# VectorE's read of one kept number takes a second operand from PSUM, at every step of left too, and not in the first 64 steps

## The chip, the cores and the metric

The kernel runs on one core of one Trainium2 chip. The metric is the time of one execution on the device, in microseconds. Besides plain runs, one execution was taken by the hardware profiler; its records are the trace, and a page summed up from them is the profile. Engines are named as in the profile: PE is TensorE's matmuls, PEld its weight loads, DVE is VectorE, ACT is ScalarE, POOL is GpSimd, SP is SyncE, which here only starts DMA transfers.

## The reference

The input `x` has the shape (4, 48, 256, 256) in float32: four images of 48 channels. Four layers are applied, each ahead of a normalization over all of an image and with the layer's input added to its output:

- Layer 0: attention between the channels, after a 3x3 depthwise convolution of queries, keys and values.
- Layer 1: a small gated unit with a depthwise convolution.
- Layers 2 and 3: "spatial message passing". The image is gone through row by row from the top (down), then from the bottom (up), then column by column from the left (right) and from the right (left). Each row or column is replaced by itself plus a convolution along it (5 taps, 48 channels to 48, and a bias) of the row or column before it, whose new value it uses: `nxt = inp + conv1d(carry)`.

The scans of layers 2 and 3 take most of the time, and what is changed lies in them. Within one direction a row can't begin before the row ahead of it is done. So a scan is a chain of some 255 small steps, four scans make a layer, and two layers follow each other.

## The kernel before, in words

**How a step is laid out.** The function `scans` (L965) works through layers 2 and 3, which it calls layer 0 and layer 1. The four images form two pairs, and each pair has its own chain, a Python generator (`chain`, L1019) that emits one step of its pair at each `yield`. Even and odd positions of a row are folded onto the partitions, so that the 48 channels become 96 partitions and the 256 positions 128, and the five taps become three matrices of 96x96. A step (`step`, L1056) treats the two images of its pair as two halves, i = 0 and i = 1. For each half, three matmuls accumulate in a PSUM tile (L1064, float32, each of two records in the trace), and VectorE adds the row of the input and writes the result to one of four `carry` tiles (L1068 in down and up, L1072 in right and left). The first half of a pair uses one PSUM bank, the second half another; each is used again at the next step. So the next step's matmuls of a half wait for the add of the same half.

**What follows a step.** The function `after` of each scan stores what the step made:

- down (L1134 to L1157): ScalarE adds the bias and writes the row in place (`keep`, L1150).
- up (L1167 to L1201): the same, at L1194.
- right (L1252 to L1298): GpSimd fetches a column out of the block ahead of time (`fetch`, L1256, the copy at L1259; two steps ahead for pair 0, three for pair 1 with its additional tile), and ScalarE writes the new column to `lines` (L1286).
- left (L1315 to L1405): GpSimd adds the new column to the image that the layer started from. In pair 1 of the last layer (`direct`) it adds half by half into tiles `done` (L1338); otherwise once per step in place into `stage` (L1334). In layer 0, VectorE takes the statistics for the next normalization from a finished block (bn_stats, L1376), one piece per step of the next block, eight pieces a block. `CB` is 16 columns, `NK` is 16 blocks.

**The read of one kept number.** After each step of down, up and right the function `look` (L1030) is called with a place of one number per partition in the tile that ScalarE (or GpSimd) has just written. It appends the place to the list `kept`. When the list is longer than three it takes the oldest, three steps old, and lets VectorE copy that number to a tile `seen` that nobody uses (L1039). In right the number is added to one of the column fetched for the next step, so that the instruction reads both (L1041). In left, at odd columns outside `direct`, VectorE copies a number of the odd column before, which GpSimd has written (L1344 to L1348). What `seen` holds plays no part in the result. The read makes VectorE wait at that place for the other engine, so that a later instruction on VectorE needs no wait of its own for it. `kept` is emptied at each block of 32 rows in down and up, and once ahead of right and of left.

**What sets the order.** The engines' instruction orders are decided by a scheduler of the framework when the program is built: instructions carry a priority by their place in the Python program, and an instruction may be moved ahead of others if its inputs come earlier in the plan. A tile that is reused makes the next writer wait for its last reader. The chains are run at L1453 to L1473: first pair 0 alone for 992 steps, with pair 1 beginning 64 steps ahead of the end of these; then both in turns; and at the end pair 1 alone, while GpSimd rearranges pair 0's result (`to_rows`, L1421, its copies at L1448). So pair 0 is alone in its first layer, both pairs are interleaved in the middle, and pair 1 is alone in most of its second layer.

Of the kernel before, what the change touches and what calls it, by code (L numbers as in the profile page):

```python
# [9 lines left out]
F32 = mybir.dt.float32  # L10
AF = mybir.ActivationFunctionType
ALU = mybir.AluOpType
# [4 lines left out]
B, C, H, W = 4, 48, 256, 256  # L17
G = 16
NP = 2
P = 96  # L20
# [944 lines left out]
def scans(ctx, tc, xs, out, wts, biases, dram, k, coefs, lead, spare):  # L965
# [13 lines left out]
    nc = tc.nc  # L979
# [8 lines left out]
    wp = pool("c_w", 1)  # L988
# [10 lines left out]
    CB = 2 * KC  # L999
# [19 lines left out]
    def chain(pair):  # L1019
# [4 lines left out]
            nc.gpsimd.memset(c, 0.0)  # L1024
        last = wp.tile([P, 2, W // 2], F32, tag=f"last{pair}", name=f"last{pair}")
        at = [0]
        seen = wp.tile([P, 1], F32, tag=f"seen{pair}", name="seen")
        kept = []

        def look(place, fetched=None):  # L1030

            kept.append(place)
            if len(kept) > 3:
                if fetched is None:
                    nc.vector.tensor_copy(seen, kept.pop(0))  # L1039
                else:  # L1040
                    nc.vector.tensor_add(seen, kept.pop(0), fetched)  # L1041

        def slot(name):
            return take(pair, f"{name}{pair}")

        def inner():
            return carry[at[0]][:, :, 1 : HP - 1]

        def advance():
            at[0] = (at[0] + 1) % NC  # L1050
            return inner()
# [4 lines left out]
        def step(layer, way, inp, after):  # L1056

            old = carry[at[0]]
            new = advance()
            for i in range(2):  # L1060
                b = slice(i, i + 1)
                ps = sums[pair].tile([P, 512], F32, tag="bank", name=f"ps{pair}{i}")[:, : W // 2]
                for j in range(3):
                    nc.tensor.matmul(  # L1064
                        ps, lhsT=w_sb[layer][:, way, j, :], rhs=old[:, i, j : j + W // 2], start=j == 0, stop=j == 2
                    )
                if len(inp.shape) == 4:
                    nc.vector.tensor_add(  # L1068
                        new[:, i].rearrange("p (k w) -> p k w", w=KC), ps.rearrange("p (k w) -> p k w", w=KC), inp[:, i]
                    )  # L1070
                else:
                    nc.vector.tensor_add(new[:, i], ps, inp[:, i])  # L1072
                after(new, b)

        def rows_view(t):
            return t.rearrange("p (b k h w) -> p b k h w", b=2, k=NK, w=KC)
# [8 lines left out]
        def row(ts, r):  # L1085
            return rows_view(ts[r % 2])[:, :, :, r // 2, :]
# [13 lines left out]
        def layer_of(layer, first):  # L1100
# [18 lines left out]
            def norm(t, b):  # L1119
                v = by_batch(t)[:, b]  # L1120
                g = biased[b]
                nc.scalar.activation(v, v, AF.Identity, bias=g[:, 1:2], scale=g[:, 0:1])
# [11 lines left out]
            for n in range(NT):  # L1134
                ahead_ = None
                for r in range(RT):
                    if r == 0:
                        kept.clear()
                        while len(halves) < min(2 * n + 5, 2 * NT):
                            t = slot("dn")  # L1140
                            load_rows(layer, len(halves) // 2, len(halves) % 2, t, 0, NK)
                            halves.append(t)
                        if n + 1 < NT:
                            ahead_ = halves[2 * n + 2 : 2 * n + 4]
                    if ahead_ and r in (11, 14, 22, 25):
                        norm(ahead_[r // 22], r % 11 // 3)
                    inp = row(now, r)

                    def keep(new, b):
                        nc.scalar.activation(inp[:, b], blocks(new[:, b]), AF.Identity, bias=bias[:, 0:1])  # L1150

                    if n == 0 and r == 0:
                        keep(inner(), slice(0, 2))
                    else:
                        step(layer, 0, inp, keep)
                    look(inp[:, 1, 0, 0:1])
                    yield  # L1157
                if ahead_:
                    for r in range(2):
                        nc.sync.dma_start(D[n][r], now[r])  # L1160
                    now = ahead_
# [5 lines left out]
            for n in reversed(range(NT)):  # L1167
                ahead_ = None
                kept.clear()
                for r in reversed(range(RT)):  # L1170
# [17 lines left out]
                    i = n * RT + r + 1  # L1188
# [63 lines left out]
            fetched = {}  # L1252
# [59 lines left out]
            direct = layer == 1 and pair == NP - 1  # L1312
            done = None
            writes = []
            for n in reversed(range(NK)):  # L1315
                ahead_ = None
                if direct and n % 2 == 1:
                    done = [take(0, "done") for _ in range(2)]
                for w in reversed(range(CB)):
                    if w == CB - 1 and n > 0:  # L1320
                        ahead_ = slot("lines"), slot("stage")
                        nc.sync.dma_start(ahead_[0], Rt[n - 1])
                        nc.sync.dma_start(by_batch(ahead_[1]), block_of(x, n - 1))
                    if layer == 0 and n == 0 and w == CB // 2:
                        following = [slot("dn"), slot("dn")]
                        for r in range(2):
                            load_rows(1, 0, r, following[r], 1, NK)
                    line = lines_view(lines)[:, w]
                    to = cols_view(stage)[:, :, w % 2, :, w // 2]

                    def keep(new, b):
                        if not direct:
                            if b.stop == 2:
                                nc.gpsimd.tensor_add(to, to, new)  # L1334
                            return
                        for i in range(b.start, b.stop):
                            place = done[i].rearrange("p (h w) -> p h w", w=2 * CB)[:, :, n % 2 * CB + w]
                            nc.gpsimd.tensor_add(place, to[:, i], new[:, i])  # L1338

                    if n == NK - 1 and w == CB - 1:  # L1340
                        keep(inner(), slice(0, 2))
                    else:
                        step(layer, 2, line, keep)
                    if not direct and w % 2:  # L1344

                        kept.append(to[:, 1, H // 2 - 1 :])
                        if len(kept) > 1:
                            nc.vector.tensor_copy(seen, kept.pop(0))  # L1348
                    if late:
                        late.pop(0)()  # L1350
                    if writes and w % 8 == 4:
                        writes.pop(0)()
                    yield
                if layer == 0:
                    nc.sync.dma_start(block_of(y, n), by_batch(stage))
                elif not direct:
                    v = stage.rearrange("p (b q t n) -> p b q t n", b=2, q=2, t=NY)
                    for b in range(2):
                        for q in range(2):
                            nc.sync.dma_start(result[:, b, :, 2 * n + q], v[:, b, q])  # L1360
                elif n % 2 == 0:

                    def write(b, r, done=done, w0=n * CB):
                        at_rows = out[(2 * pair + b) * C : (2 * pair + b + 1) * C].rearrange(
                            "c (h r w) -> c h r w", r=2, w=W
                        )
                        nc.sync.dma_start(
                            at_rows[:, :, r, w0 : w0 + 2 * CB],
                            done[b][r * C : (r + 1) * C].rearrange("c (h w) -> c h w", w=2 * CB),
                        )  # L1370

                    writes += [lambda b=b, r=r, f=write: f(b, r) for b in range(2) for r in range(2)]
                if layer == 0:

                    def stat(b, c, n=n, v=by_batch(stage)):
                        nc.vector.bn_stats(stats[b][:, n * 4 + c, :], v[:, b, c * 512 : (c + 1) * 512])  # L1376

                    late += [lambda b=b, c=c, f=stat: f(b, c) for b in range(2) for c in range(4)]
                    if n == 0:
                        for r in range(2):  # L1380
                            for q in range(2):
                                nc.sync.dma_start(
                                    rows_view(following[r])[q * C : (q + 1) * C, :, 0].rearrange("c b h w -> c b (h w)"),
                                    cols_view(stage)[r * C : (r + 1) * C, :, q, :NH, :].rearrange("c b h w -> c b (h w)"),
                                )
                if ahead_:
                    lines, stage = ahead_
# [211 lines left out]
```

## Time and profile before

| what | value |
|---|---|
| median of three runs | 9098.82 us (9097.15 to 9113.03) |
| the profiled execution itself | 9105.24 us |
| its span, first to last instruction | 9103.5 us |
| mean granted TensorE clock | 0.984 |
| busy PE / DVE / ACT / POOL | 96% / 44% / 38% / 21% |
| matmul records at L1064 | 48,960 |
| looks at L1039 / L1041 / L1348 | 1,852 / 1,008 / 381 |

The layers 0 and 1 end near 3,500 us. Then come pair 0 alone (down, up, right, left of its first layer) until about 5,000 us, both pairs until about 7,640 us, and pair 1 alone until the end, with its last right from about 8,366 us and its last left from about 8,740 us.

A line of the groups in the profile reads: line of the kernel, engine, operation, output and inputs by their names in the program, the shapes, the count, then the busy time of all in us and the mean duration in ns of one, then the idle time ahead of them on their engine and what ended most of it. Four of them that concern the change, two from the page and two from the list of groups by form:

```profile
L1041 DVE TENSOR_TENSOR seen<-lines,pre 96x1 f32<-96x1 f32 x1008 | 166.8, 165 | 479.6 <-POOL pre L1259 437.2 <-ACT lines L1286 2.3 <-DVE seen L1041 0.2
L1348 DVE COPY seen<-stage 96x1 f32<-96x1 f32 x381 | 57.0, 150 | 306.3 <-POOL stage L1334 306.3
L1039 DVE COPY seen<-dn 96x1 f32<-96x1 f32 x1040 | 148.1, 142 | 33.6 <-ACT dn L1150 19.8 <-ACT dn L1194 2.1
L1376 DVE BATCH_NORM_STATS2 st<-stage 96x6 f32<-96x512 f32 x256 | 174.3, 681 | 7.4 <-POOL stage L1334 7.3
```

The idle time ahead of the looks is spread over all stages. Where TensorE is full it costs nothing.

### The profile page before, as it was taken

Reading aid. Unit: us, or ns where it says so; the run is one execution under the profiler, and the core shown is the slowest. Engines: PE = TensorE matmul, PEld = TensorE weight load, DVE = VectorE, ACT = ScalarE, POOL = GpSimd, SP = SyncE. Lnnn points to the kernel's source line nnn. Section 1 sums busy time; section 2 is a strip of 40 time slices with the busy share of each in tenths; the row PEclk is TensorE's granted clock in tenths of the full one; section 3 lists DMA queues with packets and bytes.
Section 4 is the critical chain, followed back from the end, with each engine's and each line's share of the span. In section 5 each row is a group of like instructions: output and inputs, shape, how many; then the busy total and the mean of one; then the engine's idle time right before and its main releaser. Section 6 shows DMA issues by size and latency. Waiting matters only on the chain. (4 is left out here: it accounts for less than half of the span.)

```text
span 9103.5 us, 158554 instructions
## 1 busy us (share of the span) xinstructions
PE 8713.5 (96%) x62920; PEld 7234.4 (79%) x62920; DVE 3971.3 (44%) x14031; ACT 3440.2 (38%) x7023; POOL 1948.2 (21%) x3100
## 2 busy tenths in 40 slices
PE   6999999999999978999999999999999999999998
PEld 4777777433333336999888999999999999999998
DVE  3232010234555555444345544444444555444543
ACT  0011000123343455765400776666554002765610
POOL 0000000001111120002444000001445664001566
PEclk9999999999999988999999999999999999999999
DMA  7664323467878877765466755465556787867789
GB/s 150 132 133 89 71 62 73 94 137 168 180 171 179 180 159 163 161 143 143 119 168 165 168 140 135 116 152 134 161 158 163 215 224 175 204 168 191 210 171 184
DMA packets 1180201, 1390.37 MB, mean 153 GB/s; under 512 B 263184, under 2 KB 1107216, under 8 KB 1118784
## 3 DMA queue, kind: packets, MB, share of 16 engines
q1 hardware_dynamic: 1179360, 1379.90, 64.9%
q8 instruction: 493, 8.08, 0.4%
q14 instruction: 252, 2.06, 0.1%
q0 software_dynamic: 96, 0.33, 0.0%
HBM read 811.21 MB, written 509.61 MB: 145 GB/s over the span
## 5 line engine op out<-in xcount | busy, mean ns | idle before, releaser
L1064 PE MATMUL ps<-carry,w 96*96 96x128 f32 x48960 | 5490.2, 274 | 115.0 <-DVE carry L1072 71.7
L1064 PEld LDWEIGHTS ps<-carry,w 96*96 96x96 f32 x48960 | 5407.4, 163 | 207.4 <-DVE carry L1072 134.7
L1259 POOL COPY pre<-col 96x256 f32<-96x256 f32 x1020 | 656.7, 644 | 2755.5 <-DMA col<-last 1971.7
L1150 ACT ACTIVATE dn<-carry,b 96x128 f32<-96x128 f32 (+1 forms) x2044 | 769.1, 398 | 838.3 <-DVE carry L1068 828.9
L1286 ACT ACTIVATE lines<-carry,b 96x128 f32<-96x128 f32 (+1 forms) x2044 | 780.2, 399 | 690.8 <-DVE carry L1072 650.1
L1068 DVE TENSOR_TENSOR carry<-ps,dn 96x128 f32<-96x128 f32 x2280 | 652.5, 287 | 755.8 <-PE ps L1064 730.5
L1194 ACT ACTIVATE up<-carry,b 96x128 f32<-96x128 f32 x1792 | 719.1, 402 | 459.8 <-DVE carry L1068 456.3
L1068 DVE TENSOR_TENSOR carry<-ps,up 96x128 f32<-96x128 f32 x1792 | 516.0, 288 | 598.9 <-PE ps L1064 594.1
L1334 POOL TENSOR_TENSOR stage<-stage,carry 96x256 f32<-96x256 f32 x768 | 656.2, 856 | 527.4 <-DVE carry L1072 497.5
L1072 DVE TENSOR_TENSOR carry<-ps,lines 96x128 f32<-96x128 f32 x2040 | 547.6, 283 | 424.9 <-PE ps L1064 401.1
L581 PE MATMUL py<-x1n,wy 128*96 128x512 f32 x1536 | 703.6, 607 | 30.4 <-ACT x1n L541 27.9
L1072 DVE TENSOR_TENSOR carry<-ps,pre 96x128 f32<-96x128 f32 x2040 | 550.9, 284 | 271.1 <-PE ps L1064 239.7
L295 PE MATMUL acc<-xs,xt 128*96 128x288 f32 x2048 | 666.7, 407 | 0.0
L294 PE MATMUL acc<-xt 128*96 128x288 f32 x2048 | 666.5, 409 | 0.0
L581 PEld LDWEIGHTS py<-x1n,wy 128*96 128x96 f32 x1536 | 245.2, 166 | 455.2 <-issue 437.0
L279 DVE COPY xt<-pt 128x384 f32<-128x384 f32 x256 | 136.6, 554 | 850.8 <-PE pt L276 650.3
L261 ACT ACTIVATE xn<-raw,coef 96x2048 f32<-96x2048 f32 x64 | 133.6, 2094 | 987.6 <-PE pt L276 819.6
L296 PE MATMUL acc<-xt,xs 128*96 128x192 f32 x2048 | 501.7, 327 | 0.0
L296 PEld LDWEIGHTS acc<-xt,xs 128*96 128x96 f32 x2048 | 332.1, 165 | 154.3 <-issue 1.4
L295 PEld LDWEIGHTS acc<-xs,xt 128*96 128x96 f32 x2048 | 332.0, 164 | 151.2 <-issue 2.2
L604 DVE TENSOR_TENSOR y<-py,t 96x512 f32<-96x512 f32 x256 | 171.4, 678 | 600.8 <-PE py L590 600.8
L1041 DVE TENSOR_TENSOR seen<-lines,pre 96x1 f32<-96x1 f32 x1008 | 166.8, 165 | 479.6 <-POOL pre L1259 437.2
(183 smaller groups left out, 5520.3 us busy)
## 6 DMA issues: line engine op xcount, KB each, us to landing
stage<-x SPq DMA_DIRECT2D x64, 1536.0 KB
dn<-x SPq DMA_DIRECT2D x240, 384.0 KB
R<-lines SPq DMA_DIRECT2D x60, 1536.0 KB
lines<-R SPq DMA_DIRECT2D x60, 1536.0 KB
D<-dn SPq DMA_DIRECT2D x56, 1536.0 KB
up<-D SPq DMA_DIRECT2D x56, 1536.0 KB
U<-up SPq DMA_DIRECT2D x224, 384.0 KB
col<-U SPq DMA_DIRECT2D x56, 1536.0 KB
```

The source lines that it names most:

```text
L294: nc.tensor.matmul(acc[0], lhsT=xt[:, h + 2, :], rhs=xt[:, here, :], start=first, stop=last)
L295: nc.tensor.matmul(acc[1], lhsT=xt[:, h + 2, :], rhs=xs[:, here, :], start=first, stop=last)
L296: nc.tensor.matmul(acc[2], lhsT=xs[:, h + 2, :], rhs=xt[:, past, :], start=first, stop=last)
L581: nc.tensor.matmul(ps, lhsT=held["w"][0][:, dx], rhs=x1n[:, 2 * c : 2 * c + 2, dx : dx + W], start=dx == 0, stop=False)
L1064: nc.tensor.matmul(ps, lhsT=w_sb[layer][:, way, j, :], rhs=old[:, i, j : j + W // 2], start=j == 0, stop=j == 2)
L1068: nc.vector.tensor_add(new[:, i].rearrange("p (k w) -> p k w", w=KC), ps.rearrange("p (k w) -> p k w", w=KC), inp[:, i])
L1072: nc.vector.tensor_add(new[:, i], ps, inp[:, i])
L1150: nc.scalar.activation(inp[:, b], blocks(new[:, b]), AF.Identity, bias=bias[:, 0:1])
L1194: nc.scalar.activation(place[:, b], blocks(new[:, b]), AF.Identity, bias=bias[:, 1:2])
L1259: nc.gpsimd.tensor_copy(t, cols_view(block)[:, :, w % 2, :, w // 2])
L1286: nc.scalar.activation(line[:, b], new[:, b], AF.Identity, bias=bias[:, 2:3])
L1334: nc.gpsimd.tensor_add(to, to, new)
```

## The change

`seen` becomes two tiles in turns. `step` keeps a handle on the PSUM tile of its second half, `held["ps"]`. `look` no longer copies the old number alone: it adds to it the first number of that PSUM tile (in right, a scalar_tensor_tensor adds the PSUM number, the fetched number, which stands as a scalar operand read through a pointer, and the kept one). So a look can't be placed ahead of its own step's matmuls, and it becomes a reader of the PSUM bank. In left, `look` is called at every step in place of the copy at each second one: with a number of `done` in `direct`, and otherwise of `stage`, three steps old. In down of the first block of 32 rows and the second, for pair 0 in layer 0, no look is made. What the kernel computes stays the same.

```diff
-        seen = wp.tile([P, 1], F32, tag=f"seen{pair}", name="seen")
+        seen = [wp.tile([P, 1], F32, tag=f"seen{pair}{i}", name="seen") for i in range(2)]
         kept = []
+        held = {}
 
         def look(place, fetched=None):
             kept.append(place)
             if len(kept) > 3:
+                seen.append(seen.pop(0))
                 if fetched is None:
-                    nc.vector.tensor_copy(seen, kept.pop(0))
+                    nc.vector.tensor_add(seen[0], held["ps"][:, 0:1], kept.pop(0))
                 else:
-                    nc.vector.tensor_add(seen, kept.pop(0), fetched)
+                    nc.vector.scalar_tensor_tensor(
+                        seen[0], held["ps"][:, 0:1], fetched, kept.pop(0), ALU.add, ALU.add
+                    )
...
                     nc.vector.tensor_add(new[:, i], ps, inp[:, i])
                 after(new, b)
+            held["ps"] = ps
...
-                    look(inp[:, 1, 0, 0:1])
+                    if pair or layer or n > 1:
+
+                        look(inp[:, 1, 0, 0:1])
...
-                    if not direct and w % 2:
-
-                        kept.append(to[:, 1, H // 2 - 1 :])
-                        if len(kept) > 1:
-                            nc.vector.tensor_copy(seen, kept.pop(0))
+                    if direct:
+                        look(done[1].rearrange("p (h w) -> p h w", w=2 * CB)[:, 0, n % 2 * CB + w : n % 2 * CB + w + 1])
+                    else:
+                        look(to[:, 1, 0:1])
```

## The prediction

> **What bounds the kernel now.** I read the page first, then the matmuls of the scans cut by stage, then the chain of waits inside the stages that lose TensorE time. First line of the page's part 1:
>
> ```profile
> PE 8713.5 (96%) x62920; PEld 7234.4 (79%) x62920; DVE 3971.3 (44%) x14031; ACT 3440.2 (38%) x7023; POOL 1948.2 (21%) x3100
> ```
>
> TensorE is busy 96% of the span, so a VectorE edit can only matter where TensorE waits. The windows view, for L1064 alone, columns: window, its length, TensorE busy (records), weight loads, granted clock, DMA share, GB/s.
>
> ```profile
> 3600.00:4150.00 550.00, 549.60 (x5017) 548.85 (x5016) 1.00 0.67 149
> 4188.00:4580.00 392.00, 369.08 (x3042) 338.87 (x3041) 1.00 0.51 138
> 4604.00:4976.00 372.00, 339.27 (x2855) 315.57 (x2854) 1.00 0.63 175
> 5100.00:7600.00 2500.00, 2498.36 (x22781) 2493.07 (x22780) 1.00 0.63 160
> 7950.00:8350.00 400.00, 400.00 (x3652) 399.44 (x3651) 1.00 0.75 183
> 8400.00:8720.00 320.00, 315.31 (x2854) 312.39 (x2853) 1.00 0.74 206
> 8740.00:9080.00 340.00, 324.50 (x2846) 321.06 (x2844) 0.98 1.04 190
> ```
>
> A step is 12 records (2 halves, 3 matmuls, 2 records each). In the full stages a record takes 550/5017 = 0.1096 us, and 0.1094 in the mean of the three full rows, so a step takes 1.312 us. Row 1 (pair 0 alone, down and up), row 4 (both pairs) and row 5 (pair 1 alone, down and up) are full. Row 2 (pair 0 alone, right) runs 392/3042 x 12 = 1.546 us per step, row 3 (pair 0 alone, left) 1.564, row 6 (pair 1 alone, right) 1.3455, row 7 (pair 1's last left) 1.434. Three stages of a few hundred us lose time. The waits of pair 0's right and of its left (waiting engine, line, releaser; total us, times, longest):
>
> ```profile
> DVE seen L1041 <- POOL pre L1259: 152.1, 189, 1.1
> PEld ps L1064 <- DVE carry L1072: 37.7, 95, 0.7
> ```
> ```profile
> DVE seen L1348 <- POOL stage L1334: 88.7, 112, 1.0
> PEld ps L1064 <- DVE carry L1072: 59.8, 119, 0.7
> ```
>
> VectorE stands at a look until GpSimd delivers, the adds of the step queue behind it, and TensorE waits for the adds. The timeline of pair 0's left shows it in order of time (start, duration, idle before in brackets):
>
> ```profile
> 4750.26 0.15 DVE L1348 COPY seen<-stage 96x1 f32<-96x1 f32 x1 [0.97 <-POOL stage L1334]
> 4750.33 0.47 DVE L1072 TENSOR_TENSOR carry<-ps,lines 96x128 f32<-96x128 f32 x2
> 4750.66 2.65 PEld L1064 LDWEIGHTS ps<-carry,w 96*96 96x96 f32 x24 [0.60 <-DVE carry L1072]
> ```
>
> The two adds start only after the look, and the next weight load 0.40 us after it. In the list of instructions in built order the looks stand up to two steps ahead of the step that wrote them, hence so late a value.
>
> The full stages have hardly any room. In pair 1's up:
>
> ```profile
> 8201.04 0.29 DVE L1068 TENSOR_TENSOR carry<-ps,up 96x128 f32<-96x128 f32 x1 [0.37 <-PE ps L1064]
> 8201.25 0.14 DVE L1039 COPY seen<-up 96x1 f32<-96x1 f32 x1
> ```
>
> An add waits for three matmuls and frees the same half's next three. From the weight load at 8200.08 (start of that half) to the add is 0.96 us, the add 0.29, from its end to the next load of that half 0.053: 1.305 against the 1.312 that TensorE needs. After a load that came late the first part was 0.939. So 7 ns are free, and up to 25 ns more where the load itself is late.
>
> **What the Trainium skill says.** "Perfetto Trace Analysis", section "Identifying Dependency Chains": an instruction that waits on several engines may get a semaphore instruction in front. The trace agrees: 21 ns each on VectorE, 51 ns each on TensorE (16 of them at L1064). "PSUM — Partial Sum Buffer", section "PSUM bank collisions raise a hardware error": engines may not touch a bank at the same moment. No run here shows a collision, but the built program shows the wait that keeps it off: the next matmul into a bank waits for the bank's last reader, which after the change is the look. "VectorE: DVE Perf Modes", section on the TRN2 errata, prices a float tensor_tensor at (N+151)/0.96 ns: 158 for one element, 291 for 128. The trace has 155 alone and 284 to 288.
>
> **Part by part.** The new look stands, in built order, right behind its step's second-half add, and reads a value three steps old.
>
> *A. Down and up of a pair alone (some 850 steps).* The look lengthens the second half's cycle by its tail past the add. An add directly behind another VectorE instruction is pipelined: L1041's one-number add ends 0.067 us after the add before it (a copy 0.059). I take 0.067, since adds from PSUM run at the same duration as the formula for SBUF. New cycle 0.939 + 0.288 + 0.067 + 0.053 = 1.347, minus 1.312 = 0.035; x 850 = +30 us. Bounds of the tail: 0.060 (no dearer than a copy: +24) to 0.110 (PSUM read not pipelined: +66).
>
> *B. Pair 1's right (252 steps).* The look becomes a scalar_tensor_tensor with a pointer scalar. Nearest rows: L837 of this form takes 749 ns, L787's tensor_tensor of the same shape 686, so 63 more, which I take though the shapes are larger. Tail 0.067 + 0.063 = 0.130, cycle 1.410. Against 1.3455: +0.0645 x 252 = +16, and some 2 for GpSimd's output copies (L1448, 1133 ns) that still delay a fetch: +18. If the pointer is free: +2.5.
>
> *C. Pair 1's last left (252).* It has no look before; now one per step, but no add waits for GpSimd any longer (before, 17.5 us of idle ahead of these adds was GpSimd's `done`). It is held by loads (DMA share 1.04). +1, bounds -8 and +9.
>
> *D. Pair 0's right (252).* The wait of 152 us goes: the number fetched was released two steps before. Step 1.537 in its undisturbed part, 1.410 after: -0.127 x 252 = -32. With a free pointer -48.
>
> *E. Pair 0's left of layer 0 (15 blocks of 16 steps).* Before, a block takes 26.54 us (with one step of pair 1 slipped in). After: 16 x 1.347 = 21.55, pair 1's step 1.31, and bn_stats, 8 a block at 681 ns. Two of them now stand right behind a look and wait for GpSimd's 856 ns add of the same step, with the next add behind them; by hand, from end of add to bn_stats' end to next add, against the time at which that add was due, 1.2 + 0.75 us, the other six 0.5: 2.5. Sum 25.36, -1.2 x 15 = -18. Bounds: -55 (these stalls absorbed) and 0.
>
> *F, G, first 64 steps.* Looks in down and up that waited for ScalarE (L1039: 38 us of idle, mostly hidden): -3. Dropping the first 64 steps' looks, 61 x 0.14 us plus their waits, mostly under other work: -4. The interleaved stage is full of matmuls while VectorE is under half busy, so 570 more looks and 1,412 more VectorE semaphore instructions (21 ns) hide there: 0, +-8. There are 1,779 more semaphore instructions on TensorE's queue; the one in the trace's full stage cost nothing, since the queue runs ahead; alone each stands where the load waits anyhow. 0, upper bound 1,779 x 0.051 = +90, little believed.
>
> Sum: 30 + 18 + 1 - 32 - 18 - 3 - 4 + 0 = -8. The profiled execution took 9105.24 us (span 9103.5), so 9097 in its own terms. It stood 6.4 above the median of the runs, 9098.82, so the forecast is **9091 us**.
>
> **Rivals.**
> *Faster.* E's bn_stats waits are absorbed (-55, not -18): VectorE has 0.37 us between adds, and before the change blocks with bn_stats were hardly longer than those without. Then -8 - 37 = -45, 9054. With a free pointer as well, about -77, 9022. Against: a wait of 0.9 us doesn't fit in 0.37.
> *Slower.* The tail of a look that reads PSUM. It is in the cycle of every step of a pair alone: 850 + 252 + 252 + 240 = 1,594 steps, 16 us for each 0.010 us. At 0.110, A +66, B +29, D -21, E -7, the rest -6: +61, 9160. It decides from 0.072 (no change) and passes +0.2% at 0.083. For it: no look of a PSUM number is in the trace. Against: adds from PSUM cost as the SBUF formula says.
> *The wait only moves.* In pair 0's right and left the step takes as long as before, since a bn_stats, or the fetch, stands where the look did: D and E 0, so -8 + 32 + 18 = +42: 9141. Against it: the fetch is released two steps ahead, so only E can go this way.
>
> **How the numbers follow.** About 0.2% (18 us) is what a measurement of this kernel tells from no change. My forecast's own case (A to G near the values taken, 9081 to 9117) 0.34; the faster rival, with a free pointer or a short tail, 0.36 in all; slower by tail, TensorE's semaphores or a wait that moves, 0.30. Single cases: forecast 0.34, bn_stats absorbed 0.20, free pointer or short tail 0.16, long tail 0.16, semaphores on TensorE 0.05, wait moves 0.09. The range 9040 to 9150 leaves out the end of the faster (both gains at once) and of the slower (tail above 0.105, semaphores). The forecast's own range is 9070 to 9110.
>
> **What would show it.** Right: in the windows, pair 0's right at 1.40 us per step and no wait of the look for `pre`; down and up of one pair at 1.347; pair 1's right at 1.40; pair 0's left near 25.4 us a block with bn_stats waiting for `stage`. TensorE waits, in the full stages, for `seen` instead of `carry`. Wrong: down and up still at 1.312 (the tail is hidden) or at 1.38 (A mis-sized); the interleaved stage below 22,700 records in 2500 us (semaphores count); pair 0's right still above 1.5.

## The result and the profile after

The changed kernel takes 9115.58 us in the median of 19 runs (9107.34 to 9129.05), the kernel before 9099.31 (9091.97 to 9113.03, 19 runs). The ratio is 1.0017 with a 95% interval of 1.001 to 1.0025: slower by 16 us. The difference is under the 0.2% that the prediction took for the limit of what can be told, but with 19 runs of each the interval leaves out no change, and the forecast of 9091 lay on its other side. The profiled execution has a span of 9108.0 us.

The first line of the page shows what was added, some 570 VectorE instructions, while every engine's share stays nearly as it was:

```profile
PE 8768.0 (96%) x62920; PEld 7256.0 (80%) x62920; DVE 4071.7 (45%) x14604; ACT 3483.1 (38%) x7023; POOL 1948.4 (21%) x3100
```

The same windows as before, for the scans' matmuls alone (window, length, TensorE busy and records, weight loads, clock, DMA share, GB/s):

```profile
3600.00:4150.00 550.00, 549.52 (x4712) 524.59 (x4710) 1.00 0.63 139
4188.00:4580.00 392.00, 391.88 (x3370) 375.01 (x3370) 1.00 0.54 143
4604.00:4976.00 372.00, 361.22 (x3143) 350.16 (x3142) 1.00 0.73 192
5100.00:7600.00 2500.00, 2495.70 (x22754) 2492.41 (x22753) 1.00 0.66 163
7950.00:8350.00 400.00, 393.06 (x3367) 375.09 (x3367) 0.99 0.69 167
8400.00:8720.00 320.00, 319.21 (x2732) 303.88 (x2731) 1.00 0.68 191
8740.00:9080.00 340.00, 323.40 (x2812) 319.42 (x2810) 0.98 1.02 187
```

Read the counts, not the busy time. In the first row TensorE is as busy as before (549.5 of 550 us), and yet it ran 4,712 records where it had run 5,017: the ends of the matmuls are modelled, and such an end covers the wait of 0.1 us. The busy time of the weight loads does show it (524.59 us, before 548.85). Twelve records are a step, so 550/4712 x 12 = 1.401 us in place of 1.316.

| stage | before, us per step | forecast | after |
|---|---|---|---|
| down and up, pair 0 alone | 1.316 | 1.347 | 1.401 |
| right, pair 0 alone | 1.546 | 1.410 | 1.396 |
| left, pair 0 alone (with bn_stats) | 1.564 | 1.49 | 1.420 |
| both pairs, records in 2500 us | 22,781 | 22,781 | 22,754 |
| right, pair 1 alone | 1.3455 | 1.410 | 1.406 |
| last left, pair 1 | 1.434 | 1.44 | 1.451 |

(The forecast for left is the predicted block of 25.36 us over its 17 steps, pair 1's among them, as the windows count them too.)

To see where the time went, I set the n-th matmul record of the scans of one trace against the n-th of the other: the start after the change less the start before, in us from each span's start. The rows end at round counts, so each holds some steps of its neighbours.

| up to | records | after less before | gained or lost since the row above |
|---|---|---|---|
| first matmul of the scans | 0 | -10.5 | (layers 0 and 1, which the change doesn't touch; -11.5 to +5.3 in the traces of the ten experiments) |
| end of the first 64 steps | 1000 | -15.0 | -4.5 |
| pair 0 down and up | 6000 | +20.3 | +35 |
| pair 0 right | 9000 | -12.9 | -33 |
| pair 0 left | 13000 | -55.8 | -43 |
| both pairs | 37000 | -61.7 | -6 |
| pair 1 down and up | 43000 | -19.3 | +42 |
| pair 1 right | 46000 | -3.7 | +16 |
| pair 1 last left | 48959 | +5.3 | +9 |

Without the first row's -10.5, which lies ahead of every edit, the sum is +16, the difference of the medians. The gains of right and left, 76 us, are larger than forecast (50); down and up lose 77, and 30 were forecast. The waits of right and left show what was gained. Of pair 0's right (4188 to 4580 us), the longest wait of GpSimd within the stage:

```profile
POOL pre L1268 <- DVE seen L1045: 188.8, 249, 1.4
```

The 152 us in which VectorE stood at the look for GpSimd's column are gone; now GpSimd waits for VectorE, which costs nothing here (in experiment 8 the same stage runs at TensorE's own rate). The groups of the new looks, from the list by form:

```profile
L1045 DVE SCALAR_TENSOR_TENSOR seen<-ps,pre,lines 96x1 f32<-96x1 f32 x1008 | 206.2, 205 | 3.7 <-DVE carry L1078 3.5 <-issue 0.2
L1043 DVE TENSOR_TENSOR seen<-ps,up 96x1 f32<-96x1 f32 x812 | 117.4, 145 | 1.0 <-DVE carry L1074 0.2
L1043 DVE TENSOR_TENSOR seen<-ps,stage 96x1 f32<-96x1 f32 x759 | 109.6, 144 | 0.6 <-DVE carry L1078 0.3
```

Their idle time is 3.7, 1.0 and 0.6 us. Before, 479.6 and 306.3 us lay ahead of the looks of right and left. The PSUM operand isn't dear either: from the end of the add to the end of the look behind it is 0.066 us (median of 2,768), forecast 0.067, and 0.125 for the scalar_tensor_tensor with a pointer scalar, forecast 0.130.

What is new on TensorE is a semaphore instruction, one that only waits. It is in the list of the matmul line's instructions (count, shortest, median and longest duration in ns, first and last start), 16 times before and 1,795 times after:

```profile
L1064 PEldq EVENT_SEMAPHORE  x16: 51/51/51, 3487.2 to 8369.8; - x16
```
```profile
L1070 PEldq EVENT_SEMAPHORE  x1795: 51/51/51, 3476.6 to 8349.6; - x200
```

Followed in the records of the stages with one pair alone: without such an instruction the weight load starts 53 ns after the look's end (median of some 950, in right and left); with one it starts 115 ns after it (some 820, in down and up): 40 ns until the semaphore instruction starts, its 51, and 25 more. It stands behind the look, on the cycle, and adds 62 ns. The cycle of the prediction with it is 0.939 + 0.288 + 0.066 + 0.115 = 1.408, and 1.401 was measured.

### The profile page after: what moved, and what is told of

It reads as the page before. It is cut to its first block, busy times and chain, and to the rows that moved or that the text cites. A ratio compares the mean times of both kernels' runs of the same rounds, so it can differ in the third digit from the quotient of the medians.

```text
span 9108.0 us, 163117 instructions
## 1 busy us (share of the span) xinstructions
PE 8768.0 (96%) x62920; PEld 7256.0 (80%) x62920; DVE 4071.7 (45%) x14604; ACT 3483.1 (38%) x7023; POOL 1948.4 (21%) x3100
## 5 line engine op out<-in xcount | busy, mean ns | idle before, releaser
L1070 PE MATMUL ps<-carry,w 96*96 96x128 f32 x48960 | 5558.6, 275 | 64.2 <-DVE carry L1074 29.8
L1295 ACT ACTIVATE lines<-carry,b 96x128 f32<-96x128 f32 (+1 forms) x2044 | 819.1, 402 | 630.8 <-DVE carry L1078 621.2
L1074 DVE TENSOR_TENSOR carry<-ps,dn 96x128 f32<-96x128 f32 x2280 | 654.4, 288 | 844.2 <-PE ps L1070 823.5
L1078 DVE TENSOR_TENSOR carry<-ps,pre 96x128 f32<-96x128 f32 x2040 | 586.0, 287 | 671.8 <-PE ps L1070 670.8
L1078 DVE TENSOR_TENSOR carry<-ps,lines 96x128 f32<-96x128 f32 x2040 | 577.0, 286 | 586.0 <-PE ps L1070 578.0
L1074 DVE TENSOR_TENSOR carry<-ps,up 96x128 f32<-96x128 f32 x1792 | 515.7, 288 | 642.2 <-PE ps L1070 641.6
L590 PE MATMUL py<-x2n,wy 64*96 64x512 f32 x1536 | 363.0, 601 | 0.0
```

What stands on the lines that cost most here:

```text
L1070: nc.tensor.matmul(ps, lhsT=w_sb[layer][:, way, j, :], rhs=old[:, i, j : j + W // 2], start=j == 0, stop=j == 2)
L1074: nc.vector.tensor_add(new[:, i].rearrange("p (k w) -> p k w", w=KC), ps.rearrange("p (k w) -> p k w", w=KC), inp[:, i])
L1295: nc.scalar.activation(line[:, b], new[:, b], AF.Identity, bias=bias[:, 2:3])
```

## The experiments

Theory S after this reading: the semaphore instruction costs its time because it waits for the look on the path that sets the step. Rivals: T, the tail of the look costs all of it; V, VectorE's own additional instructions delay the adds. Ratios are to the kernel before, with their 95% intervals; steps come from windows of each run's trace.

**1. The semaphore instruction away.** In the built program it comes with the form of the add in down and up, whose view of the PSUM tile is not the one that the matmul writes by. With one view for both it vanishes. The load that it precedes waits for two things in the changed kernel, VectorE and an earlier matmul of TensorE's own; with one view the second wait is gone, and the load waits for VectorE alone.

```diff
+                q = lambda t: t.rearrange("p (k w) -> p k w", w=KC) if len(inp.shape) == 4 else t
                 for j in range(3):
                     nc.tensor.matmul(
-                        ps, lhsT=w_sb[layer][:, way, j, :], rhs=old[:, i, j : j + W // 2], start=j == 0, stop=j == 2
+                        q(ps),
+                        lhsT=w_sb[layer][:, way, j, :],
+                        rhs=q(old[:, i, j : j + W // 2]),
+                        start=j == 0,
+                        stop=j == 2,
                     )
```

> The changed kernel with one edit: the matmuls of down and up write their PSUM tile through the same rearranged view as the add reads it. In the built program the 1,779 semaphore instructions ahead of the second half's first matmul in down and up are gone; the look, its PSUM operand and the wait for it stay. Theory S (the semaphore instruction on TensorE stands in series behind the look): down and up of a pair alone fall from 1.401 us per step to 1.347, what the tail alone makes; some 890 steps x 0.054 = -48 us, 9068. Rival T (the tail of the PSUM read alone costs 0.089 past what TensorE hides, the semaphore costs nothing): 1.401 stays, 9116. Rival V (VectorE's own additional instructions delay the adds): 1.401 stays, 9116.

Measured: 0.9956 (0.9941 to 0.9971), 9055.67 us. Windows of its trace, columns as above, pair 0's down and up and its right:

```profile
3600.00:4150.00 550.00, 549.70 (x4908) 546.39 (x4907) 1.00 0.66 145
4188.00:4560.00 372.00, 372.00 (x3199) 355.90 (x3198) 1.00 0.55 147
```

Down and up take 550/4908 x 12 = 1.345 us, what the prediction had for the tail alone. Right has next to no such instructions in either and stays at 1.395 (in the same window of the changed kernel 1.3985). S holds, T and V fall: 0.056 of the 0.085 us are the semaphore instruction, 0.029 the tail. By records the two stages of down and up lose 25 us in this run and 77 in the changed kernel, so the instruction is 52 us of the time; without it the change is a gain of 0.44%.

**2. The semaphore instruction added in right and left.**

```diff
-                    nc.vector.tensor_add(new[:, i], ps, inp[:, i])
+                    q = lambda t: t.rearrange("p (k w) -> p k w", w=KC)
+                    nc.vector.tensor_add(q(new[:, i]), q(ps), q(inp[:, i]))
```

> The changed kernel with one edit: the add of right and left is written with the rearranged view that down and up have. This puts a semaphore instruction on TensorE ahead of the second half's first matmul in right and left too (3,795 in place of 1,794 in the scans); look and tail stay. Theory S: the steps of right and left of a pair alone, 1.396 (pair 0 right), 1.406 (pair 1 right), get longer by 0.055 to 0.063; 252 + 252 steps and most of the 490 in left, so +45 to +60 us: 9160 to 9175. Down and up stay at 1.401. The stage with both pairs stays full, since TensorE's queue runs ahead there. Rivals T and V: nothing changes, 9116.

Measured: 1.007 (1.0055 to 1.0085), 9156.5 us, some 4 us under the expected range.

```profile
3600.00:4150.00 550.00, 549.52 (x4708) 524.13 (x4707) 1.00 0.65 142
4188.00:4560.00 372.00, 371.88 (x3067) 341.25 (x3066) 1.00 0.52 138
5100.00:7550.00 2450.00, 2449.23 (x22375) 2447.57 (x22374) 1.00 0.64 161
```

Pair 0's right goes from 1.395 to 1.456 us, +0.060, with the same look and tail; down and up stay. In the stage with both pairs (third row) lie 1,767 of these instructions, and a record takes 2450/22375 = 0.1095 us, as before: there they cost nothing. They do wait there as well, and start some 40 ns after the end of a look as elsewhere. But TensorE's sequencer has run ahead: in the median the semaphore instruction ends 1.22 us, eleven weight loads, before the load that it guards, and meanwhile TensorE works off the matmuls that stand ahead of it. In down and up of one pair it ends 0.026 us before its load. So the price depends on whether its wait is on the path, not on its number. S again.

**3. The look reads the new carry in SBUF in place of PSUM.**

```diff
-            held["ps"] = ps
+            held["ps"] = new[:, 1]
```

> The changed kernel with one edit: the look's second operand is the first number of the second half of the new carry tile in SBUF, which this step's add has just written, in place of the number in PSUM. The look stays behind its step's second add and VectorE runs as many instructions, but it is no reader of a PSUM bank, so TensorE waits for the add alone. Theories S and T (the cost is the wait of the bank's next matmul): down and up alone back to 1.312 us, right of both pairs to 1.312 to 1.33, pair 0's left below 1.38: -80 - 45 - 15 = 8975, between 8960 and 9000. Rival V (VectorE's instructions, or the place of the look): down and up stay at 1.39 or more, 9100 to 9120.

Measured: 1.0048 (1.0031 to 1.0065), 9139.05 us, some 165 us above what was expected. Down and up did go to 550/4997 x 12 = 1.321 us, so V falls there and the wait for the bank is what matters. But pair 0's right takes 1.459 us, its left 1.556, pair 1's right 1.455. The timeline of pair 0's right (start, duration) and the groups show why:

```profile
4352.90 0.65 POOL L1268 COPY pre<-col 96x256 f32<-96x256 f32 x1 [0.96 <-DVE carry L1078]
4352.92 0.65 DVE L1045 SCALAR_TENSOR_TENSOR seen<-carry,pre,lines 96x1 f32<-96x1 f32 x1
4353.49 0.61 DVE L1078 TENSOR_TENSOR carry<-ps,pre 96x128 f32<-96x128 f32 x2
```
```profile
L1045 DVE SCALAR_TENSOR_TENSOR seen<-carry,pre,lines 96x1 f32<-96x1 f32 x1008 | 635.5, 630 | 127.1 <-ACT lines L1295 0.5
L1043 DVE TENSOR_TENSOR seen<-carry,stage 96x1 f32<-96x1 f32 x759 | 534.3, 704 | 58.9 <-DVE carry L1078 2.3
L1043 DVE TENSOR_TENSOR seen<-carry,up 96x1 f32<-96x1 f32 x812 | 131.4, 162 | 84.9 <-ACT up L1203 0.9
```

The look of one number takes 630 and 704 ns beside GpSimd's copy and add (642 and 853), and 162 in up, where GpSimd mostly rests, so that reading the new carry is not dear in itself. Of some 990 looks of right that started with or inside an operation of GpSimd, the median ends 16 ns after that operation. With one of the operands in PSUM (after) the same looks take 205 and 144. The Trainium skill says so: "SBUF — State Buffer", section "SBUF: two separate sides", has VectorE (with two SBUF inputs) and GpSimd share a pair of ports under an exclusive lock, where the later one "fully blocks". The numbers of this run agree.

**4. The change in down and up alone.** The kernel before with those two stages of the change (of its edits only the lines of `look` are shown):

```diff
                 if fetched is None:
-                    nc.vector.tensor_copy(seen, kept.pop(0))
+                    nc.vector.tensor_add(seen[0], held["ps"][:, 0:1], kept.pop(0))
                 else:
-                    nc.vector.tensor_add(seen, kept.pop(0), fetched)
+                    nc.vector.tensor_add(seen[0], kept.pop(0), fetched)
```

> The kernel before with the change in down and up alone (PSUM operand, two seen tiles, no look in the first 64 steps); right and left as before. If the parts add up: down and up of a pair alone at 1.401 us, 890 steps x 0.087 = +77, less 4 for the first 64 steps: 9172. Right and left of pair 0 stay at 1.546 and 1.564, pair 1's right at 1.3455. If part of the loss belongs to how the two parts meet (the look of right behind that of up), it is under 9150.

Measured: 1.0104 (1.0089 to 1.0119), 9191.1 us, 19 more than expected. Down and up take 1.402 us. By records it loses 36 and 46 us in the two stages of down and up (82, where 77 were expected), right and left of pair 0 run as before (within some 1 us), and 12 are lost in the last left, where nothing was edited. Down and up lose no less without the new looks of right and left, so the loss isn't made where the parts meet.

**5. Left as before.**

```diff
-                    if direct:
-                        look(done[1].rearrange("p (h w) -> p h w", w=2 * CB)[:, 0, n % 2 * CB + w : n % 2 * CB + w + 1])
-                    else:
-                        look(to[:, 1, 0:1])
+                    if not direct and w % 2:
+                        kept.append(to[:, 1, H // 2 - 1 :])
+                        if len(kept) > 1:
+                            nc.vector.tensor_copy(seen[0], kept.pop(0))
```

> The changed kernel with left as before: a copy of a kept number at each second step outside the last left, no look in the last left. If the left part is worth what the two traces show (pair 0's left 0.144 us per step less, 15.5 blocks of 16, about -36 to -40; the last left +5 to +9): pair 0's left back at 1.56 us per step, 9116 + 38 - 7 = 9147. If the gain of pair 0's left came from elsewhere (its right, DMA timing), its left stays at 1.42 and the time at 9110.

Measured: 1.0071 (1.0056 to 1.0086), 9161.78 us. Pair 0's left runs 1,851 records in 240 us where the changed kernel runs 2,045 in the same window: 1.556 us per step against 1.408. Its gain is the new look's. The time is 15 us above what was expected: by records the stage with both pairs loses 8 us too, where pair 1's left of its first layer has the old look again, and the last left gives nothing back. It loses 9 us against before, without any look in it; with experiment 4 this shows that the loss there isn't the look's. What it is stays open: the DMA share of the stage is 1.0, and its start has moved.

**6. A longer tail in down and up.** The kept number twice, as the pointer scalar too:

```diff
-                if fetched is None:
+                if way == "du":
+                    kept_ = kept.pop(0)
+                    nc.vector.scalar_tensor_tensor(seen[0], held["ps"][:, 0:1], kept_, kept_, ALU.add, ALU.add)
+                elif fetched is None:
...
-                        look(inp[:, 1, 0, 0:1])
+                        look(inp[:, 1, 0, 0:1], way="du")
...
-                    look(place[:, 1, 0, 0:1])
+                    look(place[:, 1, 0, 0:1], way="du")
```

> The changed kernel with one edit: in down and up the look is a scalar_tensor_tensor with a pointer scalar (the kept number twice) in place of the tensor_tensor. In right this form's tail past the add was 0.125 us against 0.066. If the tail is on the path one to one: down and up alone from 1.401 to 1.460 us per step, 890 x 0.059 = +52: 9168. If the semaphore instruction alone sets the step (the tail is covered by it): 1.401 stays, 9116.

Measured: one run, 9161.97 us. Down and up run 4,534 records in the window of 550 us: 1.456 us, +0.055 for a tail longer by 0.059. The tail is on the path too, in series with the semaphore instruction.

**7. Four banks for pair 1.**

```diff
-    psum = pool("c_psum", 2, space=PSUM)
+    psum = pool("c_psum", 4, space=PSUM)
```

> The changed kernel with one edit: pair 1's PSUM pool has four banks in place of two, so a bank is written again two steps later; pair 0 keeps two. In the built program pair 1's semaphore instructions on TensorE vanish with it, pair 0's stay. If the loss is the wait for the bank: pair 1's down and up go to 1.312 us, its right from 1.406 to 1.312 or up to 1.33, pair 0's down and up stay at 1.401; -42 - 20 = 9053. If it is the VectorE work: pair 1 as pair 0, 9116.

Measured: one run, 9050.09 us. Pair 1's down and up: 2,558 records in 280 us, 1.314 us; its right 1,557 in 170, 1.310. Pair 0, with two banks, stays at 4,712 in 550, 1.401. One trace has both cases, with the same looks: the loss is the wait for the bank, with the semaphore instruction that belongs to it.

**8. More banks for both pairs.** Pair 1 has three, pair 0 from step 64 on two more in turns with its own:

```diff
-    psum = pool("c_psum", 2, space=PSUM)
-    sums = [spare, psum]
+    psum = pool("c_psum", 3, space=PSUM)
+    more = pool("c_more", 2, space=PSUM)
+    sums = [spare, psum]
+    after64 = [Ring([spare, more]), psum]
+    steps = [0, 0]
...
-                ps = sums[pair].tile([P, 512], F32, tag="bank", name=f"ps{pair}{i}")[:, : W // 2]
+                ps = (sums if steps[pair] < 64 else after64)[pair].tile([P, 512], F32, tag="bank", name=f"ps{pair}{i}")[:, : W // 2]
...
             held["ps"] = ps
+            steps[pair] += 1
```

> The changed kernel with more banks for both pairs: pair 1 has three, pair 0 two of its own and from step 64 on two more in turns. The look keeps its PSUM operand, and so its place, but no matmul waits for it. Down and up alone at 1.312 us in both pairs, pair 0's right at 1.312 to 1.33 (1.396), its left at 1.35 (1.42), pair 1's right at 1.312 to 1.33 (1.406): 9116 - 77 - 18 - 15 - 20 = 8986, between 8970 and 9000, 1.2% under the kernel before. If VectorE's work costs something of its own: above 9030.

Measured: 0.9872 (0.9853 to 0.9891), 8981.28 us, faster than both kernels. Pair 0's down and up, its right, and pair 1's right:

```profile
3600.00:4150.00 550.00, 549.75 (x5014) 549.23 (x5013) 1.00 0.69 149
4188.00:4530.00 342.00, 342.00 (x3128) 341.94 (x3127) 1.00 0.61 161
8300.00:8560.00 260.00, 260.00 (x2379) 260.00 (x2378) 1.00 0.75 211
```

All three are at 1.31 to 1.32 us per step, TensorE's own rate. Left of pair 0 takes 1.389 us where 1.35 was expected (1.408 in the same window of the changed kernel); bn_stats still waits for GpSimd there.

**9. The banks alone,** added in the same way to the kernel before.

> The kernel before with the additional PSUM banks of the fastest version and nothing else. Theory (the gain is the place of the look; the banks only take the wait away that its PSUM operand brings): no change, 9099 plus or minus 8, right and left of pair 0 stay at 1.546 and 1.564 us per step. Rival (the banks give the gain, since TensorE runs further ahead): pair 0's right and left get shorter, under 9060.

Measured: 0.9995 (0.9986 to 1.0004), 9092.98 us. No change that the measurement tells; pair 0's right takes 1.544 us per step and its left 1.561 in this trace, as before. So the gain of the eighth experiment is the new look's, and the banks take away its price. In right the look reads the same numbers as before and one in PSUM, so what is left is its place and its form; the two `seen` tiles do nothing there by themselves (experiment 4 has them, with right at 1.534). In left the number read is also one step older than before, and no run parts that from the place.

**10. The look from the first step on,** in the kernel of the eighth experiment.

```diff
-                    if pair or layer or n > 1:
-
-                        look(inp[:, 1, 0, 0:1])
+                    look(inp[:, 1, 0, 0:1])
```

> The fastest version (look with PSUM operand, more banks) with the look from the first step on, as before the change, in place of from step 64 on. If leaving the first 64 steps' looks out is worth something, this is 4 us slower or more (8981 to 8986 and above, since layers 0 and 1 still run beside these steps); if not, the times agree within some 5 us.

Measured: 0.9913 (0.9899 to 0.9928), 9022.22 us, some 40 us slower. At record 0 its trace is level with that of before; the 48th record comes 237 us late, the 1000th 34. The first look stands at 3531.3 us:

```profile
L1046 DVE TENSOR_TENSOR seen<-ps,dn x1040: 134/143/155, 3531.3 to 7987.8; 96x1 f32<-96x1 f32 x174
```

On VectorE 259 instructions of the reference's layer 1, the gated unit, lie between the chain's eighth add and this look, and the ninth add comes behind it (the 2,334th instruction of VectorE, where it is the 2,065th in the eighth experiment). In the kernel before the first look stood as late, at 3553.3 us, but no matmul waited for it. Here the step that waits for this look's bank waits with it, and TensorE's gaps in layer 1 stay empty: 73 us busy in 3350 to 3450, against 88 with the looks left out. So leaving the first 64 looks out is no small part of the change: it keeps a look that is tied to a PSUM bank from holding the start back. (In these 64 steps the eighth experiment has the banks of the changed kernel; that the changed kernel would lose as much was not run.)

## Why the prediction was wrong

The path was right: the look in the cycle of the second half's bank, GpSimd's waits gone from right and left. One term was put at nothing for a reason that doesn't hold, and another was sized at less than half. By the steps of the prediction:

- **A, the tail in down and up.** Forecast +30, tail 0.067, step 1.347. With the semaphore instruction away, experiment 1 has 1.345 us per step, and the records give +12 and +14 us in the two stages. Right. The step of 1.38 or more, which the prediction named as the sign of a mis-sized A, did come (1.401), but through G.
- **G, the semaphore instructions on TensorE.** This is the step that failed: "alone each stands where the load waits anyhow. 0". Where the load waits, the instruction waits as well, for the same look, and runs its 51 ns after the wait's end, not beside it, with 11 ns more since two hand-overs (40 and 25 ns) stand in place of one (53). Measured 0.056 us per step by experiment 1 and 0.060 by experiment 2, +52 us. The upper bound of +90 had stood in the prediction, but was reckoned over all 1,779 of them, with "little believed"; it should have been those that stand in down and up of one pair alone, some 830, and believed. Those of the stage with both pairs, some 870, cost nothing, as forecast, and for the forecast's reason: the queue has run ahead (experiment 2). The price stood in the trace before: 12 of its 16 start 38 to 40 ns after the end of the add that they wait for, and the load follows 24 or 25 ns behind their 51, so some 115 ns after the add in place of 53.
- **B and D, right.** +16 against +18, and -33 to -38 against -32. Right, with 0.059 us for the scalar_tensor_tensor with a pointer scalar, where 0.063 was taken. (How much of it is the pointer's, no run shows.)
- **E, pair 0's left.** -38 (15 blocks x 2.56) against -18. The two stalls behind a waiting bn_stats were sized rightly: counted from one first-half add to the next, these steps take 2.55 and 2.05 us in the trace after, where undisturbed ones take 1.34, so 1.21 and 0.71 more for the forecast's 1.2 and 0.75. But a block takes 23.98 us (mean of 13), not 25.36. The difference is pair 1's step, which I had added at 1.31 us. It falls into the same stretch, where TensorE waits for VectorE:

```profile
4613.33 1.27 DVE L1384 BATCH_NORM_STATS2 st<-stage 96x6 f32<-96x512 f32 x2
4614.52 0.57 DVE L1078 TENSOR_TENSOR carry<-ps,lines 96x128 f32<-96x128 f32 x2
4615.78 0.29 DVE L1078 TENSOR_TENSOR carry<-ps,lines 96x128 f32<-96x128 f32 x1
4615.98 0.28 DVE L1074 TENSOR_TENSOR carry<-ps,dn 96x128 f32<-96x128 f32 x1
```

  L1074's adds are pair 1's here, and the steps around them take 1.26, 1.31 and 1.53 us, together 0.08 more than three undisturbed ones.
- **C, the last left.** +9 against +1, within its bound; experiments 4 and 5 show that it isn't the look's, and its cause stays open.
- **F and the first 64 steps.** -4.5 for -7, and -6 for 0 in the stage with both pairs, within its bounds. VectorE has 2,190 more semaphore instructions in the trace (4,518, before 2,328), not 1,412. Experiment 10 shows more: without the edit of the first 64 steps the change would have cost some 40 us more, at least with more banks.

Sum, by the rows of the table of records: the semaphore instructions (+52) and C (+8) against the additional gain in left (-25, of which some 20 in the blocks) and small terms (some -11 among A, B, D, F and the stage with both pairs) make the 24 us between 9091 and 9115. That the miss is no larger is luck: two errors of opposite sign met. Had the semaphore instruction been priced, the forecast would have been 9143 with E as it stood, and some 9120 with E right. Of the rivals, the slower one was right on the place (the look's path to the second half's next load in every step of a pair alone) and wrong on the part: not the tail at 0.110, but what stands behind it.

## What to carry to other kernels

An instruction that reads a PSUM bank joins the cycle of that bank, however small it is: price its tail and what the wait for it adds in front of the next matmul, once for each turn of the cycle, or give the chain more banks (here 1.4% of the changed kernel's time, and nothing for the kernel before). Ask of every wait that is added whether a semaphore instruction comes with it, and whether it waits on the path: here those off the path were free, and those on it cost their duration and a second hand-over. In this kernel a read without work that only orders an engine was best with one PSUM operand while GpSimd ran beside it, and best left out where its place would have held back a chain that had just begun. And before a new cost is put at nothing, look in the trace before for the few places where it stands already.

## What the runs showed of the hardware

Three things that I had not expected. A semaphore instruction on TensorE that waits on the path adds 62 ns (53 to 115 from look to load), more than its 51; one that ends 1.22 us ahead of its load adds nothing. In left a VectorE instruction on one number takes 144 ns with a PSUM operand and 704 (mean) with two SBUF operands, while GpSimd works on SBUF. And TensorE's busy time did not show a wait of some 0.09 us per step: it stayed at 549.5 of 550 us while 6% of the records were gone.
